# A two-layer graph attention kernel: superchunks of 26 chunks in place of 24, the carried row in row 0 of the node block, one scan penalty for all heads

## The chip, the core and the metric

The kernel runs on one core of one Trainium2 chip. The metric is the device time of one launch in microseconds (us); less is better. The engines are named as in the profile: PE (TensorE matmul; PEld is its weight load), DVE (VectorE), ACT (ScalarE), POOL (GpSimd) and SP (SyncE, which here issues nearly all plain DMAs). Ln is line n of the kernel before, unless the text says otherwise.

## What is computed

A graph with N = 6250 nodes of 256 features and E = 200000 edges, sorted by destination, each with 32 edge attributes. Two graph attention layers, with 4 heads of 64 and 1 head of 256, follow a layer norm with ReLU. The reference, cut:

```python
def _gat(x, src, dst, ea, Wg, a_s, a_d, Wge, a_e, b, n, h, f):
    hx = (x @ Wg).reshape(n, h, f)
    he = (ea @ Wge).reshape(-1, h, f)
    al = leaky_relu(einsum('nhf,hf->nh', hx, a_s)[src] + einsum('nhf,hf->nh', hx, a_d)[dst]
                    + einsum('ehf,hf->eh', he, a_e), 0.2)
    m = segment_max(al, dst, num_segments=n)
    al = exp(al - m[dst])
    al = al / segment_sum(al, dst, num_segments=n)[dst]
    out = segment_sum(hx[src] * al[:, :, None], dst, num_segments=n)
    return out.reshape(n, h * f) + b

# h = relu(layernorm(x)); each layer l, with self loops added to the edges (their edge term is
# the mean of te over the node's edges):
te = relu(edge_attr @ We_l + be_l) * exp(x @ Wo_l + bo_l)[src][:, None]
x0 = relu(_gat(h, ..., HEADS=4) + h);  x1 = _gat(x0, ..., 1) + x0;  result = x + x1 + h
```

## The kernel before, in words

**Tiles and steps.** The sorted edges are cut into 1563 chunks of 128 edges, and these into superchunks of C = 24 chunks (`cuts`, L46): 64 of 24, one of 14 and one of 13. One superchunk is one step of a layer, so there are 66 steps in layer 0 and 66 in layer 1. The nodes that a superchunk's edges lead to lie side by side and are fewer than 128, so a step owns a block of up to 128 node rows that begins at its first destination, `base`.

**The prologue** norms x, multiplies it by the layer's weights and writes the table T0: 268 numbers for each node, the row that an edge gathers. It works on groups of GT = 7 node tiles (after a first group of 2): DVE takes statistics, ACT norms (`h`, L303), PE turns and multiplies, DVE adds the bias into one of three `trow` buffers (L428), SP stores the group to T0 (L328). Step 0's 24 chunks are gathered from x itself, before T0 is there (`NX` = 24, L243). Between these lines a generator of index work is woven in; SP loads `drow` (L441), the destinations with one row per superchunk, and `r` (L443, tile `r4`), and DVE makes `lrow` from drow (L468), which goes to `locrow` in DRAM, and from r4 the link flags (L481 to L489).

**A step** (`edges`, L611 on) is an order written out by hand, and each engine runs its instructions in that order:

- POOL gathers the next step's G rows, one indirect DMA per chunk (`gather`, L928), with a memset of a tile `gap` after each (L932). G has three buffers, so gather(k+3) waits for the sums of step k.
- PE multiplies the edge attributes (y, L1014; ACT's ReLU R, L1019) and adds the destination term by a one-hot product (zad, L1028, L1073, L1087). DVE turns the result round (rt, L1101; ade, L1104), adds the gathered term (al, L1115 to L1121) and runs the maximum along each destination's edges: two scans along the chunk (L1128, L1130), whose penalties `pen` restart the scan where the destination changes, links over the partitions (L1148, L1150) and the maxima (L1165 to L1192).
- DVE scales G (L1223, 6.5 us) and builds the one-hot S from `loc`, the edge's destination less `base` (L1058, 3.3 us). PE then adds up S x G over the chunks, two matmuls each, into u (L1234), and ACT copies u to U (`evict`, L1239).
- A destination whose edges go on in the next superchunk must hand its partial sums over. `carry` (L1241) picks the last node's row of U with a matmul by the column `lsel` (PE fin, L1245) and copies it to row 0 of a tile (ACT, L1247); `carried` (L1197) adds it, rescaled, to the first edge of the next step before that step's sums.
- `finish` merges the self loop and normalizes. In layer 0, `rows1` to `rows3` multiply the block by the next layer's weights and store the 128 rows of table T1 (`t1row`, L1370). In layer 1 the block goes to the output (L1375), for the last two steps by an indirect DMA from POOL (L1379).
- `nodes` (L989) loads the block's own rows two steps ahead: `tw` from the table (L995), and in layer 0 also the x rows (L997). Edge attributes `ea` and the bytes `lb` come for two steps at once (L955), link flags `fl` for four (L980), indices `gi` for four (L554).

Neighbouring blocks overlap by the rows that do not belong to them; later stores overwrite these in order. Layer 1's first gather waits for the last T1 store. The last four steps of a layer run in two other orders (`tight`, `last`), in which no further gather of the same layer is left to wait for.

**Scan penalties.** `pen` holds 4 numbers for each chunk, one per head, all the same: DVE computes the first head's, and ACT copies it for the three others, once per group of four steps (L598).

Of the kernel before, what the change touches and what calls it, by code (L numbers as in the profile page):

```python
# [31 lines left out]
P = 128  # L32
C = 24
SE = P * C
NX = 24
D = 256
# [9 lines left out]
def cuts(E):  # L46

    n = -(-E // P)
    k = -(-n // C)
    if k == 1:  # L50
        return [n]
    rest = n - C * (k - 2)
    return [C] * (k - 2) + [rest - rest // 2, rest // 2]

# [24 lines left out]
class Kernel:  # L79
# [31 lines left out]
    def consts(self, wp):  # L111
# [35 lines left out]
        self.kps = k = self.ps_k.tile([P, 512], F32, name="kps")  # L147
        V.tensor_copy(k[:, 0:P], self.iota_f)
        m32 = wp.tile([P, 1], F32, name="m32", bufs=1)
# [6 lines left out]
        V.tensor_add(k[:, P:P + 1], self.iota_p, m32)  # L156
        self.k_iota, self.k_part, self.k_w = k[:, 0:P], k[:, P:P + 1], k[:, 2 * P:2 * P + 4 * C + 4]
        self.wea = []
# [38 lines left out]
    def prologue(self):  # L197
# [3 lines left out]
        NT = -(-N // P)  # L201
        GT = 7
        CX = self.CX = min(self.cs[0], NX)
# [226 lines left out]
    def indices(self, wp):  # L430
# [28 lines left out]
        self.qsel = cp.tile([P, NS, 4], F32, name="qsel")  # L459
        V.tensor_scalar(self.qsel.rearrange("p s k -> p k s"), qd, self.iota_p, None, op0=OP.add)  # L460
        yield
# [35 lines left out]
        yield  # L497
        ll = wp.tile([P, NS], F32, name="ll", bufs=1)
        V.tensor_sub(ll, last, base)
        self.lsel = cp.tile([P, NS], F32, name="lsel")  # L500
        V.tensor_scalar(self.lsel, ll, self.iota_p, None, op0=OP.is_equal)
        yield
# [6 lines left out]
        V.memset(chk, 0.0)  # L509
        V.tensor_scalar(chk[:, 0, :NS], ll[0:1, :], float(P - 1), None, op0=OP.is_gt)  # L510
        V.tensor_sub(qd[0:1], qlast[0:1], qbase[0:1])
# [5 lines left out]
        V.tensor_sub(nb[:, :NS], nb[:, 1:], nb[:, :NS])  # L517
        V.tensor_scalar(chk[:, 1, :NS], nb[:, :NS], float(P), None, op0=OP.is_gt)
        V.tensor_scalar(chk[:, 2, :NS], nb[:, :NS], 0.0, None, op0=OP.is_lt)
# [11 lines left out]
    def index_tiles(self):  # L531
        cp, cs, NS, NCH = self.cp, self.cs, self.NS, self.NCH

        self.groups = []
        for s in range(NS):
            g = self.groups[-1] if self.groups else None
            if g and cs[g[0]] == cs[s] and len(g) < 4:
                g.append(s)
            else:
                self.groups.append([s])  # L540
        self.src = cp.tile([P, NCH], I32, name="src")
        self.loc, self.fpen, self.lpen, self.isl = (cp.tile([P, NCH], BF, name=n)
                                                    for n in ("loc", "fpen", "lpen", "isl"))
        self.pen = cp.tile([P, 4 * NCH + 1], BF, name="pen")
        self.bad = cp.tile([P, 1 + len(self.groups)], F32, name="bad")
# [11 lines left out]
    def index_group(self, g, pool, di):  # L557
# [23 lines left out]
        for pen, e in zip((self.fpen, self.lpen), ends):  # L581
# [5 lines left out]
            yield  # L587
        pv = self.pen[:, 4 * o:4 * (o + w)].rearrange("p (s h c) -> p s h c", h=4, c=c)
        t = pool.tile([P, 4 * C], F32, name="gt", bufs=2)
# [3 lines left out]
        yield  # L593
        V.tensor_scalar(pv[:, :, 0, :], t3, 1.0, -BIG, op0=OP.min, op1=OP.mult)
        V.memset(self.pen[:, 4 * (o + w):4 * (o + w) + 1], -BIG)
        yield
        for h in range(1, 4):
            nc.scalar.activation(pv[:, :, h, :], pv[:, :, 0, :], AF.Copy)  # L598
            yield
        t = pool.tile([P, 4 * C], F32, name="gt", bufs=2)  # L600
# [10 lines left out]
    def edges(self, ctx):  # L611
# [12 lines left out]
        self.state = {0: None, 1: None}  # L624
        self.early = 0
        self.nodes(steps[0])
        self.gather(steps[0], self.CX)
# [16 lines left out]
        for k, st in enumerate(steps):  # L644
# [51 lines left out]
            if enter:  # L696
                pr = pv
            else:
                self.evict(st)
                self.carry(st)  # L700
                if pv:
                    self.rows1(pv)
                    late = pv
# [23 lines left out]
    def tight(self, st, pv, pr, nx):  # L727
# [38 lines left out]
        if final:  # L766
            self.carry(pv)
            drain(y)
            self.load_ea(st["k"] + 2)
        else:  # L770
            self.evict(pv)
        self.rphase2(nx)
        self.adst(nx)
        if not final:
            self.carry(pv)
            if pr:
                self.rows1(pr)
                self.rows2(pr)
# [10 lines left out]
    def last(self, st, pv, nx):  # L789
# [21 lines left out]
        if pv:  # L811
            self.evict(pv)
            self.carry(pv)
        drain(self.scale(st, 3))
# [174 lines left out]
    def nodes(self, st):  # L989
        nc, L, s = self.nc, st["L"], st["s"]  # L990
        r = self.row(0, s)
        tw = self.np_.tile([P, self.L[0].TW + D], F32, name="tw", bufs=5)
        st["tw"], st["xw"] = tw[:, :L.TW], tw[:, L.TW:L.TW + D]
        w = L.TW + L.l * D
        nc.sync.dma_start(tw[:, :w], self.T[L.l][ds(r, P), 0:w])  # L995
        if L.l == 0:
            nc.sync.dma_start(st["xw"], self.a["x"][ds(r, P), :])  # L997

# [6 lines left out]
    def rphase1(self, st):  # L1005
        nc, L = self.nc, st["L"]
        l, ea = L.l, st["ea"]
        st["R"] = R = self.wp.tile([P, 2, 32 * C], F32, name="R", bufs=1)
        c = st["C"]
        for i in range(2):  # L1010
            r = slice(i * PH, (i + 1) * PH)
            y = self.ps_y.tile([P, 1024], F32, name="y")
            for w, o in self.halves(st):
                nc.tensor.matmul(y[:, o], self.webd[l][r, :], ea[r, w], start=True, stop=True)  # L1014
            if c % 2:
                for w, o in self.halves(st):
                    nc.scalar.activation(R[:, i, w], y[:, o], AF.Relu, bias=self.be[l])
            else:
                nc.scalar.activation(R[:, i, :32 * c].rearrange("p (b n) -> p b n", b=2),  # L1019
                                     y.rearrange("p (b n) -> p b n", b=2)[:, :, :16 * c], AF.Relu, bias=self.be[l])  # L1020
            yield
# [9 lines left out]
    def spread(self, st):  # L1031
# [6 lines left out]
        if len(q) < 2 or q[0]["C"] != q[1]["C"]:  # L1038
# [5 lines left out]
        V.tensor_tensor(Q[:, :i].rearrange("p i (k j) -> p (i k) j", j=32),  # L1044
                        self.k_iota[:, 0:32].unsqueeze(1).to_broadcast([P, 4 * i, 32]),
                        self.qsel[:, s:s + i, :].rearrange("p i k -> p (i k)").unsqueeze(2)
# [4 lines left out]
    def onehots(self, st, c0=0, c1=C):  # L1051
        nc, o = self.nc, st["o"]
        c1 = min(c1, st["C"])
        if "S" not in st:
            st["S"] = self.sp.tile([P, C, P], F32, name="S")
        if c0 < c1:
            w = [P, c1 - c0, P]
# [3 lines left out]
    def parts(self, st):  # L1061
# [10 lines left out]
        st["zad"] = z = self.ps_1.tile([P, 1024], F32, name="zad")  # L1072
        self.nc.tensor.matmul(z[:, 400:400 + 3 * H], st["Q"], a3[:, :H, :].rearrange("p h t -> p (h t)"),  # L1073
                              start=True, stop=True)

    def blocks(self, st):
# [3 lines left out]
        self.nc.vector.tensor_tensor(aq[:, :, 4:4 + 3 * H],  # L1080
                                     st["zad"][:, 400:400 + 3 * H].unsqueeze(1).to_broadcast([P, 4, 3 * H]),
                                     self.quad.unsqueeze(2).to_broadcast([P, 4, 3 * H]), op=OP.mult)
# [24 lines left out]
    def logits(self, st):  # L1107
# [14 lines left out]
        yield  # L1122
        n, p0 = H * c, 4 * o
        fb, w = self.fb[st["k"] % 2], c if H > 1 else 1
        x = c - 1 + 32 * w
        st["f"], st["b"] = f, b = fb[:, :n], fb[:, x:x + n]
        st["ends"] = fb[:, c - 1:c + (31 + H) * w:w]
        V.tensor_tensor_scan(f, self.pen[:, p0:p0 + n], al[:, :n], -BIG, op0=OP.add, op1=OP.max)  # L1128
        yield
        V.tensor_tensor_scan(b[:, ::-1], self.pen[:, p0 + 1:p0 + n + 1][:, ::-1], al[:, :n][:, ::-1], -BIG,  # L1130
                             op0=OP.add, op1=OP.max)
# [65 lines left out]
    def carried(self, st):  # L1197


        if st["prev"] is not None:  # L1200
            L, V = st["L"], self.nc.vector
            H, pr = L.H, st["pr"]
            g, cv = st["G"][0:1, 0, :], st["prev"]["carry"]
            if H == 1:
# [31 lines left out]
    def evict(self, st):  # L1236
        L = st["L"]
        st["U"] = U = self.np_.tile([P, 272], F32, name="U", bufs=3)
        self.nc.scalar.activation(U[:, :L.W], st["u"][:, :L.W], AF.Copy)  # L1239

    def carry(self, st):  # L1241
        nc, L, s, U = self.nc, st["L"], st["s"], st["U"]
        if s + 1 < self.NS:
            pr = self.ps_f.tile([P, 512], F32, name="fin")
            nc.tensor.matmul(pr[0:1, :L.W], self.lsel[:, s:s + 1], U[:, :L.W], start=True, stop=True)  # L1245
            st["carry"] = cv = self.wp.tile([1, 272], F32, name="carry")
            nc.scalar.activation(cv[:, :L.W], pr[0:1, :L.W], AF.Copy)  # L1247

# [116 lines left out]
    def rows3(self, st):  # L1365
        nc, L, s = self.nc, st["L"], st["s"]
        if L.l == 0:
            self.table_row(st)
            r = self.row(0, s)
            nc.sync.dma_start(self.T[1][ds(r, P), :], st["trow"])  # L1370
            return
        o, out = st["o"], self.a["out"]
        if s < self.direct:
            r = self.row(1, s)
            nc.sync.dma_start(out[ds(r, P), :], o)  # L1375
        else:
            idx = self.np_.tile([P, 1], I32, name="oidx")
            nc.vector.tensor_add(idx, self.base_f[:, s:s + 1], self.iota_p)
            nc.gpsimd.indirect_dma_start(  # L1379
# [217 lines left out]
```

## Time and profile before

| | before |
|---|---|
| time, median of 3 runs (lowest to highest) | 4717.75 us (4715.25 to 4721.8) |
| profiled execution: its own time / its span | 4718.23 / 4716.0 us |
| granted TensorE clock, mean of the span | 0.732 |
| busy: PE / DVE / POOL / ACT | 3214.2 / 2878.5 / 3701.8 / 574.2 us |
| DMA, software queue (gathers) / hardware queue (SP) | 422.75 / 158.16 MB, 33.8% / 10.1% of 16 engines' span |
| first gather from T0 / first U / first gather of layer 1 / last U | 95.31 / 184.88 / 2419.91 / 4701.13 us |

Times of single instructions count from the start of the span. A group's line in the profile gives count, busy us and mean ns of one, then how long the engine was idle before these instructions and what ended most of that. "remote" is a releaser that the profile can't name, "issue" is time in which the engine waited for nothing that the profile shows. SPq rows are SP's DMA issues: start, how long the issue took, and what is moved.

### The profile page before, as it was taken

To read this page: it belongs to the slowest core of one execution; us is meant where nothing else is said; L and a number is where in the kernel's file an instruction comes from. 1 tells how busy PE (TensorE), PEld (TensorE's weight loads), DVE (VectorE), ACT (ScalarE), POOL (GpSimd) and SP (SyncE) were. 2 spreads that over 40 slices of the span, in tenths; PEclk is the share of its full clock that TensorE was granted. 3 is DMA by queue.
4 is the path that set the end of the run, shared out by engine and by line. 5 is a ranking of instruction groups with operands and counts; after the bars stand their busy time and mean duration, and the time that the engine had idled before them with its cause. 6 is when DMAs were issued, how large, how long until landed. Compare 5 with 4: busy or idle time off the path is not lost.

```text
span 4716.0 us, 38255 instructions
## 1 busy us (share of the span) xinstructions
PE 3214.2 (68%) x10176; PEld 1915.8 (41%) x10176; DVE 2878.5 (61%) x6552; ACT 574.2 (12%) x1282; POOL 3701.8 (78%) x6350
## 2 busy tenths in 40 slices
PE   7777767777677776777655666666666666656666
PEld 6444444444444443444422333434333343433334
DVE  7566767667676676766743555546455555645555
ACT  5111111111111111111100001000000100000010
POOL 5688888888888888888648888888888888888884
PEclk9677777767777777777866677777767776777778
DMA  6344444444444444444323444444444444444442
GB/s 216 111 129 126 136 122 129 134 122 135 127 134 127 124 136 123 132 131 124 107 84 104 128 118 126 125 112 127 120 127 118 126 126 111 127 118 128 118 124 63
DMA packets 236364, 584.09 MB, mean 124 GB/s; under 512 B 63097, under 2 KB 91007, under 8 KB 236073
## 3 DMA queue, kind: packets, MB, share of 16 engines
q0 software_dynamic: 150144, 422.75, 33.8%
q1 hardware_dynamic: 85579, 158.16, 10.1%
q8 instruction: 82, 1.34, 0.1%
q14 instruction: 143, 1.17, 0.1%
q10 hardware_dynamic: 416, 0.67, 0.1%
HBM read 547.11 MB, written 34.33 MB: 123 GB/s over the span
## 4 chain that ended last, share of the span: by engine, by line
DVE 40%; another core or an unknown queue 33%; PE 16%; issue 6%; ACT 4%; POOL 0%; DMA 0%; SPq 0%; DVEq 0%; ACTq 0%; POOLq 0%
DVE G L1223 16%; DVE S L1058 8%; PE y L1014 8%; PE fin L1245 3%; DVE rt L1101 2%; ACT R L1019 1%; ACT U L1239 1%; DVE ade L1104 1%; PE fin L1329 1%; PE u L1234 1%; PE lf L1138 1%; PE zad L1028 1%; DVE mt L1172 1%; DVE m L1175 1%
## 5 line engine op out<-in xcount | busy, mean ns | idle before, releaser
L928 POOL DMA_INDIRECT G<-T,src x3102 | 2974.0, 959 | 938.3 <-issue 498.2
L1234 PE MATMUL u<-G,S 128*128 128x270 f32 (+1 forms) x6252 | 1469.7, 393 | 110.3 <-issue 58.0
L1234 PEld LDWEIGHTS u<-G,S 128*128 128x128 f32 x6252 | 1186.9, 192 | 394.5 <-issue 87.1
L1245 PE MATMUL fin<-U,lsel 128*1 128x270 f32 (+1 forms) x260 | 132.8, 613 | 1143.3 <-ACT U L1239 1136.6
L1223 DVE TENSOR_TENSOR G<-G,kps 128x6144 f32<-128x6144 f32 (+2 forms) x140 | 853.3, 6100 | 0.0
L1014 PE MATMUL y<-ea,webd 64*128 64x384 f32 (+1 forms) x1056 | 754.6, 866 | 89.2 <-issue 65.5
L932 POOL MEMSET gap<- 128x128 f32 x3102 | 684.6, 221 | 4.3 <-remote 1.3
L1148 DVE TENSOR_TENSOR_SCAN cl<-fl,cl,lf 4x129 f32<-4x129 f32 (+1 forms) x130 | 61.2, 471 | 1016.6 <-PE zad L1073 994.3
L1245 PEld LDWEIGHTS fin<-U,lsel 128*1 128x1 f32 x260 | 11.1, 81 | 1202.6 <-ACT U L1239 1201.5
L1028 PE MATMUL zad<-R,wea 128*64 128x384 f32 (+1 forms) x1056 | 474.0, 816 | 0.3 <-DVE aq L1080 0.3
L1014 PEld LDWEIGHTS y<-ea,webd 64*128 64x128 f32 x1056 | 303.3, 317 | 360.3 <-issue 330.0
L1058 DVE TENSOR_TENSOR S<-kps,loc 128x3072 f32<-128x3072 f32 x132 | 436.2, 3305 | 0.0
L1019 ACT ACTIVATE R<-y,webd 128x768 f32<-128x768 f32 x260 | 232.9, 896 | 794.6 <-PE y L1014 348.3
L1028 PEld LDWEIGHTS zad<-R,wea 128*64 128x64 f32 x1056 | 160.4, 207 | 314.9 <-issue 248.5
L1239 ACT ACTIVATE U<-u 128x270 f32<-128x270 f32 (+1 forms) x132 | 51.8, 393 | 1627.1 <-remote 1585.4
L1101 DVE STREAM_TRANSPOSE rt<-zad 128x768 f32<-128x768 f32 (+1 forms) x130 | 125.0, 961 | 27.8 <-remote 15.7
L424 PE MATMUL fin<-wg,h1T 128*128 128x260 f32 x264 | 135.7, 669 | 3.2 <-ACT h1T L1331 3.2
L1043 DVE TENSOR_TENSOR lb<-lb,kps 128x1536 bf16<-128x1536 bf16 (+1 forms) x68 | 113.0, 1662 | 0.0
L424 PE MATMUL ps<-wg,hT 128*128 128x266 f32 x292 | 89.8, 435 | 25.4 <-ACT hT L311 13.9
L424 PEld LDWEIGHTS fin<-wg,h1T 128*128 128x128 f32 x264 | 76.0, 317 | 53.7 <-issue 36.3
L1272 ACT ACTIVATE mw<-mw,mg 128x2 f32<-128x2 f32 x66 | 19.7, 298 | 557.3 <-DVE mw L1264 249.1
L1138 PE MATMUL lf<-ident,fb 128*36 128x128 f32 (+1 forms) x132 | 54.9, 416 | 42.8 <-DVE al L1119 28.2
(193 smaller groups left out, 2269.0 us busy)
## 6 DMA issues: line engine op xcount, KB each, us to landing
G<-T,src POOLq DMA_INDIRECT x3102
ea<-in_ea_dram SPq DMA_DIRECT2D x64, 768.0 KB
lb<-locrow SPq DMA_DIRECT2D x64, 384.0 KB
T<-t1row SPq DMA_DIRECT2D x66, 260.0 KB
tw<-T SPq DMA_DIRECT2D x66, 258.0 KB
tw<-T SPq DMA_DIRECT2D x66, 134.0 KB
tw<-in_x_dram SPq DMA_DIRECT2D x66, 128.0 KB
out_dram<-fb SPq DMA_DIRECT2D x64, 128.0 KB
```

What stands on the lines that cost most here:

```text
L424: self.nc.tensor.matmul(ps[:, :L.MW], hT[:, k, :], self.wg[L.l][:, k, :], start=(k == 0), stop=(k == 1))
L928: nc.gpsimd.indirect_dma_start(out=G[:, c, 0:L.TW], out_offset=None, in_=self.rows[L.l][0:n * (1 + L.l), :], in_offset=bass.IndirectOffset ...
L932: nc.gpsimd.memset(self.gap, 0.0)
L1014: nc.tensor.matmul(y[:, o], self.webd[l][r, :], ea[r, w], start=True, stop=True)
L1019: nc.scalar.activation(R[:, i, :32 * c].rearrange("p (b n) -> p b n", b=2), y.rearrange("p (b n) -> p b n", b=2)[:, :, :16 * c], AF.Relu, ...
L1028: nc.tensor.matmul(st["zad"][i * PH:(i + 1) * PH, o], self.wea[l][0], R[:, i, w], start=True, stop=False)
L1043: V.tensor_tensor(lb[:, :, :n], lb[:, :, :n], self.k_part.unsqueeze(2).to_broadcast([P, i, n]), op=OP.is_equal)
L1058: nc.vector.tensor_tensor(st["S"][:, c0:c1, :], self.k_iota.unsqueeze(1).to_broadcast(w), self.loc[:, o + c0:o + c1].unsqueeze(2).to_broad ...
L1101: V.transpose(rv[:, :32 * c].rearrange("p (b n) -> p b n", b=2), z.rearrange("p (b n) -> p b n", b=2)[:, :, :16 * c])
L1223: nc.vector.tensor_tensor(v, v, pw[:, c0:c1, :].unsqueeze(3) .to_broadcast([P, c1 - c0, H, L.F]), op=OP.mult)
L1234: nc.tensor.matmul(st["u"][:, :L.W], S[:, i, :], G[:, i, 0:L.W], start=(j == 0), stop=(j == c - 1))
L1245: nc.tensor.matmul(pr[0:1, :L.W], self.lsel[:, s:s + 1], U[:, :L.W], start=True, stop=True)
```

## The change

- `C` is 26. `cuts` fills superchunks of 26 and splits what is left: 59 of 26, one of 15, one of 14; 61 steps per layer.
- Column 0 of the one-hot S now stands for the superchunk's last node: a 128x1 copy writes `lastloc` of the step into column 0 of the comparison row, and columns 1 to 127 compare with j - 1. So row 0 of U is the carried row, `carried` reads it there, and `carry` and `lsel` are gone. A block's nodes are rows 1 to 127, and its DMAs (`tw`, x, T1 store, output) move 127 rows. Row 0 of the four `tw` buffers (there were five) is set to zero once.
- `pen` holds one number per chunk. In each step of layer 0 an ACT copy spreads it over the four heads into `pen4`; the three copies per group (L598) are gone.
- With it go `GT` = 6 in the prologue, a column offset in `zad` (480 for 400), and row 0's index out of bounds in the last two outputs. `NX` stays 24, so two of step 0's 26 chunks are gathered from T0. The loads and tiles with one row per superchunk have 61 rows for 66.

```diff
-C = 24
+C = 26
@@ cuts
-    k = -(-n // C)
-    if k == 1:
-        return [n]
-    rest = n - C * (k - 2)
-    return [C] * (k - 2) + [rest - rest // 2, rest // 2]
+    k = n // C
+    rest = n - C * k
+    if rest < 8:
+        k, rest = k - 1, rest + C
+    return [C] * k + [rest - rest // 2, rest // 2]
@@ prologue
-        GT = 7
+        GT = 6
@@ index_tiles
-        self.pen = cp.tile([P, 4 * NCH + 1], BF, name="pen")
+        self.pen = cp.tile([P, NCH + 1], BF, name="pen")
...
+        self.pen4 = [cp.tile([P, 4 * C + 1], BF, name=f"pen4{i}") for i in range(2)]
@@ index_group
-        for h in range(1, 4):
-            nc.scalar.activation(pv[:, :, h, :], pv[:, :, 0, :], AF.Copy)
-            yield
@@ edges, tight, last
-                self.carry(st)
...
+        self.tws = [self.np_.tile([P, self.L[0].TW + D], F32, name=f"tw{i}", bufs=1) for i in range(4)]
+        for t in self.tws:
+            nc.vector.memset(t[0:1, :], 0.0)
@@ nodes
-        tw = self.np_.tile([P, self.L[0].TW + D], F32, name="tw", bufs=5)
+        tw = self.tws[st["k"] % 4]
...
-        nc.sync.dma_start(tw[:, :w], self.T[L.l][ds(r, P), 0:w])
+        nc.sync.dma_start(tw[1:P, :w], self.T[L.l][ds(r, P - 1), 0:w])
...
-            nc.sync.dma_start(st["xw"], self.a["x"][ds(r, P), :])
+            nc.sync.dma_start(st["xw"][1:P, :], self.a["x"][ds(r, P - 1), :])
@@ rphase1
+        if H > 1:
+            st["pen"] = pen = self.pen4[st["k"] % 2]
+            nc.scalar.activation(pen[:, :H * c].rearrange("p (h c) -> p h c", c=c),
+                                 self.pen[:, o:o + c].unsqueeze(1).to_broadcast([P, H, c]), AF.Copy)
+            if c < C:
+                nc.vector.memset(pen[:, H * c:H * c + 1], -BIG)
@@ onehots
             st["S"] = self.sp.tile([P, C, P], F32, name="S")
+            nc.vector.tensor_copy(self.k_iota[:, 0:1], self.lastloc[:, st["s"]:st["s"] + 1])
@@ carried
-            g, cv = st["G"][0:1, 0, :], st["prev"]["carry"]
+            g, cv = st["G"][0:1, 0, :], st["prev"]["U"]
@@ carry (removed)
-            nc.tensor.matmul(pr[0:1, :L.W], self.lsel[:, s:s + 1], U[:, :L.W], start=True, stop=True)
-            st["carry"] = cv = self.wp.tile([1, 272], F32, name="carry")
-            nc.scalar.activation(cv[:, :L.W], pr[0:1, :L.W], AF.Copy)
@@ rows3
-            nc.sync.dma_start(self.T[1][ds(r, P), :], st["trow"])
+            nc.sync.dma_start(self.T[1][ds(r, P - 1), :], st["trow"][1:P, :])
...
-            nc.sync.dma_start(out[ds(r, P), :], o)
+            nc.sync.dma_start(out[ds(r, P - 1), :], o[1:P, :])
```

More of the change, by code (lines that the diff above doesn't have):

```diff
@@ L147, in consts @@
         self.kps = k = self.ps_k.tile([P, 512], F32, name="kps")
-        V.tensor_copy(k[:, 0:P], self.iota_f)
+        V.tensor_scalar(k[:, 0:P], self.iota_f, -1.0, None, op0=OP.add)
+        V.tensor_copy(k[:, P + 2:P + 34], self.iota_f[:, 0:32])
+        self.iota_m = cp.tile([P, 1], F32, name="iota_m")
+        nc.gpsimd.iota(self.iota_m, pattern=[[0, 1]], base=-1, channel_multiplier=1,
+                       allow_small_or_imprecise_dtypes=True)
         m32 = wp.tile([P, 1], F32, name="m32", bufs=1)
@@ L156, in consts @@
         V.tensor_add(k[:, P:P + 1], self.iota_p, m32)
-        self.k_iota, self.k_part, self.k_w = k[:, 0:P], k[:, P:P + 1], k[:, 2 * P:2 * P + 4 * C + 4]
+        self.k_iota, self.k_part, self.k_32 = k[:, 0:P], k[:, P:P + 1], k[:, P + 2:P + 34]
+        self.k_w = k[:, 2 * P:2 * P + 4 * C + 4]
         self.wea = []
@@ L459, in indices @@
         self.qsel = cp.tile([P, NS, 4], F32, name="qsel")
-        V.tensor_scalar(self.qsel.rearrange("p s k -> p k s"), qd, self.iota_p, None, op0=OP.add)
+        V.tensor_scalar(self.qsel.rearrange("p s k -> p k s"), qd, self.iota_m, None, op0=OP.add)
         yield
@@ L497, in indices @@
         yield
-        ll = wp.tile([P, NS], F32, name="ll", bufs=1)
+        self.lastloc = ll = cp.tile([P, NS], F32, name="lastloc")
         V.tensor_sub(ll, last, base)
-        self.lsel = cp.tile([P, NS], F32, name="lsel")
-        V.tensor_scalar(self.lsel, ll, self.iota_p, None, op0=OP.is_equal)
         yield
@@ L509, in indices @@
         V.memset(chk, 0.0)
-        V.tensor_scalar(chk[:, 0, :NS], ll[0:1, :], float(P - 1), None, op0=OP.is_gt)
+        V.tensor_scalar(chk[:, 0, :NS], ll[0:1, :], float(P - 2), None, op0=OP.is_gt)
         V.tensor_sub(qd[0:1], qlast[0:1], qbase[0:1])
@@ L517, in indices @@
         V.tensor_sub(nb[:, :NS], nb[:, 1:], nb[:, :NS])
-        V.tensor_scalar(chk[:, 1, :NS], nb[:, :NS], float(P), None, op0=OP.is_gt)
+        V.tensor_scalar(chk[:, 1, :NS], nb[:, :NS], float(P - 1), None, op0=OP.is_gt)
         V.tensor_scalar(chk[:, 2, :NS], nb[:, :NS], 0.0, None, op0=OP.is_lt)
@@ L543, in index_tiles @@
                                                     for n in ("loc", "fpen", "lpen", "isl"))
-        self.pen = cp.tile([P, 4 * NCH + 1], BF, name="pen")
+        self.pen = cp.tile([P, NCH + 1], BF, name="pen")
+        self.nc.gpsimd.memset(self.pen[:, NCH:], -BIG)
+        self.pen4 = [cp.tile([P, 4 * C + 1], BF, name=f"pen4{i}") for i in range(2)]
+        for t in self.pen4:
+            self.nc.gpsimd.memset(t[:, 4 * C:], -BIG)
         self.bad = cp.tile([P, 1 + len(self.groups)], F32, name="bad")
@@ L587, in index_group @@
             yield
-        pv = self.pen[:, 4 * o:4 * (o + w)].rearrange("p (s h c) -> p s h c", h=4, c=c)
         t = pool.tile([P, 4 * C], F32, name="gt", bufs=2)
@@ L593, in index_group @@
         yield
-        V.tensor_scalar(pv[:, :, 0, :], t3, 1.0, -BIG, op0=OP.min, op1=OP.mult)
-        V.memset(self.pen[:, 4 * (o + w):4 * (o + w) + 1], -BIG)
+        V.tensor_scalar(self.pen[:, o:o + w], t[:, :w], 1.0, -BIG, op0=OP.min, op1=OP.mult)
         yield
-        for h in range(1, 4):
-            nc.scalar.activation(pv[:, :, h, :], pv[:, :, 0, :], AF.Copy)
-            yield
         t = pool.tile([P, 4 * C], F32, name="gt", bufs=2)
@@ L766, in tight @@
         if final:
-            self.carry(pv)
             drain(y)
@@ L774, in tight @@
         if not final:
-            self.carry(pv)
             if pr:
@@ L812, in last @@
             self.evict(pv)
-            self.carry(pv)
         drain(self.scale(st, 3))
@@ L1008, in rphase1 @@
         st["R"] = R = self.wp.tile([P, 2, 32 * C], F32, name="R", bufs=1)
-        c = st["C"]
+        c, o, H = st["C"], st["o"], L.H
+        st["pen"] = self.pen[:, o:o + c + 1]
+        if H > 1:
[4 more added lines that the diff above has]
+                nc.vector.memset(pen[:, H * c:H * c + 1], -BIG)
         for i in range(2):
@@ L1044, in spread @@
         V.tensor_tensor(Q[:, :i].rearrange("p i (k j) -> p (i k) j", j=32),
-                        self.k_iota[:, 0:32].unsqueeze(1).to_broadcast([P, 4 * i, 32]),
+                        self.k_32.unsqueeze(1).to_broadcast([P, 4 * i, 32]),
                         self.qsel[:, s:s + i, :].rearrange("p i k -> p (i k)").unsqueeze(2)
@@ L1072, in parts @@
         st["zad"] = z = self.ps_1.tile([P, 1024], F32, name="zad")
-        self.nc.tensor.matmul(z[:, 400:400 + 3 * H], st["Q"], a3[:, :H, :].rearrange("p h t -> p (h t)"),
+        self.nc.tensor.matmul(z[:, 480:480 + 3 * H], st["Q"], a3[:, :H, :].rearrange("p h t -> p (h t)"),
                               start=True, stop=True)
@@ L1080, in blocks @@
         self.nc.vector.tensor_tensor(aq[:, :, 4:4 + 3 * H],
-                                     st["zad"][:, 400:400 + 3 * H].unsqueeze(1).to_broadcast([P, 4, 3 * H]),
+                                     st["zad"][:, 480:480 + 3 * H].unsqueeze(1).to_broadcast([P, 4, 3 * H]),
                                      self.quad.unsqueeze(2).to_broadcast([P, 4, 3 * H]), op=OP.mult)
@@ L1122, in logits @@
         yield
-        n, p0 = H * c, 4 * o
+        n = H * c
+        pen = st["pen"]
         fb, w = self.fb[st["k"] % 2], c if H > 1 else 1
@@ L1127, in logits @@
         st["ends"] = fb[:, c - 1:c + (31 + H) * w:w]
-        V.tensor_tensor_scan(f, self.pen[:, p0:p0 + n], al[:, :n], -BIG, op0=OP.add, op1=OP.max)
+        V.tensor_tensor_scan(f, pen[:, :n], al[:, :n], -BIG, op0=OP.add, op1=OP.max)
         yield
-        V.tensor_tensor_scan(b[:, ::-1], self.pen[:, p0 + 1:p0 + n + 1][:, ::-1], al[:, :n][:, ::-1], -BIG,
+        V.tensor_tensor_scan(b[:, ::-1], pen[:, 1:n + 1][:, ::-1], al[:, :n][:, ::-1], -BIG,
                              op0=OP.add, op1=OP.max)
@@ L1239, in evict @@
         self.nc.scalar.activation(U[:, :L.W], st["u"][:, :L.W], AF.Copy)
[L1241 to L1245, printed above, removed]
-            st["carry"] = cv = self.wp.tile([1, 272], F32, name="carry")
-            nc.scalar.activation(cv[:, :L.W], pr[0:1, :L.W], AF.Copy)
     def merge(self, st, wp, w):
@@ L1374, in rows3 @@
             r = self.row(1, s)
-            nc.sync.dma_start(out[ds(r, P), :], o)
+            nc.sync.dma_start(out[ds(r, P - 1), :], o[1:P, :])
         else:
             idx = self.np_.tile([P, 1], I32, name="oidx")
-            nc.vector.tensor_add(idx, self.base_f[:, s:s + 1], self.iota_p)
+            nc.vector.tensor_add(idx, self.base_f[:, s:s + 1], self.iota_m)
+            nc.vector.memset(idx[0:1, :], 1 << 20)
             nc.gpsimd.indirect_dma_start(
```

## The prediction

> **What bounds the kernel now.** I read the busy times first, then the waits, then one step of the timeline, then the order of SP's transfers. The page's first section and three of its groups (columns: count, busy us and mean ns, idle us before them with its releaser):
>
> ```profile
> PE 3214.2 (68%) x10176; PEld 1915.8 (41%) x10176; DVE 2878.5 (61%) x6552; ACT 574.2 (12%) x1282; POOL 3701.8 (78%) x6350
> ...
> L928 POOL DMA_INDIRECT G<-T,src x3102 | 2974.0, 959 | 938.3 <-issue 498.2
> ...
> L1245 PE MATMUL fin<-U,lsel 128*1 128x270 f32 (+1 forms) x260 | 132.8, 613 | 1143.3 <-ACT U L1239 1136.6
> ...
> L932 POOL MEMSET gap<- 128x128 f32 x3102 | 684.6, 221 | 4.3 <-remote 1.3
> ```
>
> POOL is the busiest. Its gathers cost 0.95 us, the gap memset 0.22 and the issue 0.17, 1.34 us a chunk. The waits of POOL and ACT (us in total, times, longest):
>
> ```profile
> POOL G L928 <- remote: 285.9, 120, 3.0
> POOL G L928 <- DMA T<-t1row: 69.1, 1, 69.1
> ...
> ACT U L1239 <- remote: 1585.4, 123, 58.5
> ```
>
> The 120 "remote" waits are one pause of about 2.4 us at each step's turn. The timeline shows that turn, on POOL, PE and ACT:
>
> ```profile
> 823.12 11.37 PE L1234 MATMUL u<-G,S 128*128 128x270 f32 x48 [0.49 <-issue]
> 842.61 0.61 PE L1245 MATMUL fin<-U,lsel 128*1 128x270 f32 x1 [8.12 <-ACT U L1239]
> ...
> 839.64 0.23 POOL L932 MEMSET gap<- 128x128 f32 x1
> 842.40 0.95 POOL L928 DMA_INDIRECT G<-T,src  x1 [2.54 <-remote]
> ...
> 842.16 0.40 ACT L1239 ACTIVATE U<-u 128x270 f32<-128x270 f32 x1 [9.65 <-remote]
> ```
>
> The one-hot sums are done at 834.5, yet U is copied at 842.16, 2.3 us after POOL's last memset; then POOL starts again. U follows POOL's running group and not PE's sums: a full step takes 34.60 us in layer 0 and 34.40 in layer 1, although layer 1 has 4 us less PE work and 2.4 less DVE work. So gathers pace the steps, and PE's chain has some 7.7 us (layer 0) and 10.3 us (layer 1) to spare.
>
> **Part 1: longer steps, fewer of them.** A layer had 64 steps of 24 chunks and then 14 and 13; it now has 59 of 26 and then 15 and 14. The gathers stay 3126 chunks at 1.34 us; only the pause can shrink. U comes 34.36 us after the group's first gather with 24 chunks, 18.70 with the 13 of the last step: 1.424 us a chunk and 0.19 fixed, and 0.24 more to the next first gather. So 26 chunks give 37.45 us: 59 x 37.45 against 64 x 34.60 is -4.8, and the tail's two extra chunks cost +2.8, so -2.0. Layer 1 (34.16 and 18.58) gives -2.2. Together **-4**. If instead the pause is a constant 2.4, a step is 34.60 + 2 x 1.336 = 37.27, and the two layers win 12.8 + 11.8 = 25. I take -4, which rests on two group sizes, and keep -25 for the range.
>
> **Part 2: the carried row.** PE's fin (two matmuls, 1.07 us) and ACT's copy (0.39) go. In a full step they lie inside the spare 7.7 us and are worth nothing. In the last four steps of a layer POOL runs dry and the chain sets the pace: 8 steps, of whose 1.46 us between a sixth and a half lies on it, **-4** (-2 to -6).
>
> **Part 3: small operations.** Added per step: one 128x1 DVE copy, about 0.14 us by L1258's row; per layer-0 step one ACT copy of the penalties, 0.27 by L598's. ACT is 12% busy and DVE's step has 12 us idle. One-hots and scale grow by 26/24 (3.3 to 3.6 and 6.5 to 7.1). All lie under the spare 7.7; without that cover they would cost about 1.3 us a step. Zero. Step 0 gathers two chunks more from T (2.7 us), inside POOL's 9.8 us wait for U at 185.62.
>
> **Part 4: 127 and 61 rows.** The node transfers (tw, x, the T1 store, the output) now have 127 rows, and the loads with one row per superchunk (`drow`, `r4`, `bcol`) 61 instead of 66. The trace's transfer records show how rows spread. 128 rows of 1072 B ran in 0.8 us, 16 or more at once; `r4`'s 66 rows ran at most 11 at once; but the 106-row zero store (L235) began with a row every 45 ns, one after another, and took 3.84 us. Row counts with small divisors get few engines: 128 has 16, 66 has 11, 106 has 2; 127 and 61 are prime. I take one engine for both. The Trainium skill, "DMA: Bandwidth & Descriptors", section "Why a DMA increments its semaphore by 16 and not by 1", says just this: the largest number up to 16 that divides the dimension, with 127 rows on 1 as an example, always the lowest-numbered engine. By it every one of these transfers shares one engine; the 106 rows agree.
>
> On one engine, by rows of this trace (46 ns for 1024 B, 48 for 1072, 85 for 2080): tw 6.1 us, x 5.8, T1 store 10.8 in layer 0; tw 10.8 and out 5.8 in layer 1. Four costs follow.
>
> *Prologue.* SP's order there:
>
> ```profile
> 30.05 0.35 SPq L441 DMA_DIRECT2D drow<-in_drow_dram  x1
> 30.44 0.34 SPq L443 DMA_DIRECT2D r<-in_prow_dram  x1
> ...
> 35.14 0.34 SPq L328 DMA_DIRECT2D T<-trow  x1
> 35.58 0.38 SPq L218 DMA_DIRECT2D x<-in_x_dram  x1
> ```
>
> A `drow` row of 12288 B took 460 ns at best, 775 in the mean. 61 rows of 13312 B one behind another are 30 to 51 us; `r4` adds 61 x 0.155 to 0.19, 10 to 12 us. What SP queues behind them (a T0 store, x tiles) has a share on that engine, and lands only at 76 to 100. DVE, which computes lrow from drow at 46.89 (L468), stops there; then the trow buffer of the store issued at 35 is wanted again for tile 18, which DVE wrote at about 51.6. That is 24 to 48 us late; some 5 us of ACT's waits for POOL's ln values vanish in the stall: 19 to 48. The other engines' transfers end early, so rows should run near their best: **+28**. The gathers of T wait for this chain (ACT h, at 95.31), so nothing hides it.
>
> *Start.* tw and x for steps 0 to 2 leave at 143.7 to 147.3. The first lands 6.1 instead of 0.8 us after its start, and DVE's parts(0) reads it at 145.87: +5 to +9, **+6**.
>
> *Layer boundary.* POOL waits 69.1 us for the last T1 store, issued at 2417.05 and 12 us after the one before it; the gather starts at 2419.91. 10.8 instead of 1.0 us: **+10**.
>
> *Full steps.* In a layer-0 step this engine has 22.7 us of node rows, 1.6 of other loads, and its share of 26 gathers, two packets each: 8.6 us at 166 ns, the fastest, 13 at the mean 250, 21 at 410, the slowest tenth. That is 33 to 46 us in a step of 37.45: from nothing to 8.6 us a step, 0 to 470 for 55 steps. The transfers themselves are wanted 33 us (fl) to 47 (tw) after their issue, and POOL may run 8 gathers ahead, so lateness is hidden until the engine is full. At the mean packet it is just full: 0.3 us a step, **+16**. Layer 1 (16.6 us of rows) has room.
>
> **The sum.** Own time 4718.23 us (span 4716.0 and 2.2 around it), 0.5 above the median of the runs. -4 - 4 + 28 + 6 + 10 + 16 = +52: **4770**.
>
> **The rivals.** *Faster: the rows are spread all the same.* If 127 rows get 16 engines in shares of 8 and 7, as 128 do, part 4 falls away and 4689 (constant pause) to 4710 is left. For it: SP's queue never shows an engine number. Against: the 106 rows. It decides as soon as tw lands within 2 us.
>
> *The one engine overflows.* If gather packets on it take the loaded 410 ns, gathers of layer 0 wait for its share and a step takes 46 us: 4754 + 55 x 8.6, about 5230; at 300 ns (15.6 us of gathers, 39.9 in all) 2.5 us a step, 4890. Against: the mean of 250, and a slowed engine leaves fewer packets in flight elsewhere.
>
> *The pause is constant.* 4749 with the other terms, 4721 if these are at their low ends (19, 5, 10, 0, and -6 for the tails). For it: the pause is 2.45 and 2.36 us in both layers.
>
> *PE or DVE becomes the bound.* It would need 7.7 us of growth in a layer-0 step; the sums' two chunks add 0.95, y and zad about 0.4, DVE 0.9. Against.
>
> **How the numbers follow.** Forecast 0.48 (4735 to 4800); overflow 0.18 (4800 to 5230); constant pause with low costs 0.16 (4715 to 4735); rows spread 0.14 (4689 to 4710); PE or DVE 0.04. About 0.2% (9.4 us) is what a measurement of this kernel can tell from no change. Faster: the 0.14 and a little of the constant pause, 0.17. Same: most of the rest of that case, 0.10. Slower 0.73. The range leaves out the lower half of the spread case and the overflow beyond 4880: 4700 to 4880, about 0.8.
>
> **What would show it.** Right: a tw transfer that takes 6 us with its rows one after another; DVE waiting at lrow or trow near 50 to 80 us for a DMA, and POOL's first gather from T near 123; the boundary's wait 10 us longer than the stores explain before; full steps near 37.5 us, with U still 0.2 us before POOL's restart; no fin at L1245. Wrong: layer-0 steps beyond 38 us or clearly longer than layer 1's (the engine overflows); steps at 37.27 or below (constant pause); a first gather still near 95 us (rows spread, or the stall hidden).

## The result: 4800 us for 4717, slower by 1.8%

The changed kernel takes 4800.13 us (median of 4 runs, 4796.63 to 4809.32), the kernel before 4717.47 (4 runs): ratio 1.0179, 95% interval 1.0164 to 1.0194, or +82.7 us. The forecast was 4770, the range 4700 to 4880. The profiled execution is the slowest of the four, 4809.32 us; its span of 4807.3 is 91.3 longer than that of before. In the lines of a run, Ln is a line of that run's own kernel (L1244 here is L1234 before).

The page after, the same groups as before; `fin` at the carry is gone, and POOL's work is what it was:

```profile
PE 3025.5 (63%) x9676; PEld 1849.1 (38%) x9676; DVE 2812.9 (59%) x6213; ACT 490.0 (10%) x1093; POOL 3703.0 (77%) x6382
...
L929 POOL DMA_INDIRECT G<-T,src x3102 | 2967.4, 957 | 981.9 <-issue 512.1
...
L933 POOL MEMSET gap<- 128x128 f32 x3100 | 685.5, 221 | 9.4 <-remote 6.2
```

The waits after, of POOL, ACT and DVE:

```profile
POOL G L929 <- remote: 226.2, 91, 3.7
POOL G L929 <- DMA T<-t1row: 91.4, 1, 91.4
...
POOL G L929 <- ACT G L327: 25.3, 1, 25.3
...
ACT U L1249 <- remote: 1718.8, 93, 58.6
...
DVE a L1077 <- DMA tw<-T: 32.9, 2, 28.6
...
DVE lrow L473 <- DMA drow<-in_drow_dram: 21.4, 1, 21.4
...
DVE trow L433 <- DMA T<-trow: 10.4, 1, 10.4
...
DVE cl L1158 <- DMA fl<-flags: 9.5, 1, 9.5
```

The pause at a step's turn is still there, but rarer. POOL's wait for the last T1 store has grown from 69.1 to 91.4 us. New among the longer waits are DVE's for `drow`, for a T0 store and for the flags `fl`, and POOL's, 25.3 us, for an exp of ACT at the prologue's end. DVE's longest wait for a `tw` load, at the layer boundary, has grown from 3.1 to 28.6 us, but the first U of layer 1 does not come later for it: it follows the layer's first gather by 109.9 us, and by 110.8 in the split version below, where that wait is 4.8.

The timeline of one full step of layer 0, on PE, POOL and ACT:

```profile
922.54 12.12 PE L1244 MATMUL u<-G,S 128*128 128x270 f32 x52 [0.75 <-DVE G L1223]
...
945.49 0.22 POOL L933 MEMSET gap<- 128x128 f32 x1
948.46 0.95 POOL L929 DMA_INDIRECT G<-T,src  x1 [2.75 <-remote]
...
948.22 0.40 ACT L1249 ACTIVATE U<-u 128x270 f32<-128x270 f32 x1 [15.74 <-remote]
```

The sums end at 934.7, U comes at 948.22: 13.5 us now lie between them (7.7 before), so in a full step neither the larger operations nor the missing carry are on the path. SP's issues in the prologue (start, how long the issue took):

```profile
31.57 0.60 SPq L446 DMA_DIRECT2D drow<-in_drow_dram  x1
32.21 1.34 SPq L448 DMA_DIRECT2D r<-in_prow_dram  x1
33.60 33.55 SPq L449 DMA_DIRECT2D src<-in_src_dram  x1
...
71.67 1.16 SPq L333 DMA_DIRECT2D T<-trow  x1
72.88 0.75 SPq L223 DMA_DIRECT2D x<-in_x_dram  x1
```

The issue behind the two 61-row loads took 33.55 us, and the T0 store that left at 35.14 before leaves at 71.67. In the transfer records drow's 61 rows run from 35.25 to 72.78, 553 ns each, never more than two at once; the 127 rows of a tw load of layer 0 take 8.3 us in the median (5.8 to 8.7), those of a T1 store 14.4.

By stages, from the copies of U (us; the last three columns are from one other chip, on which the kernel before takes 4768; the split version is experiment 1's):

| stage | before | after | before | after | split |
|---|---|---|---|---|---|
| first gather from T0 | 95.3 | 135.2 | 94.8 | 132.3 | 103.8 |
| to the first U | 184.9 | 238.0 | 184.6 | 236.2 | 205.8 |
| first to last U of layer 0 | 2217.6 | 2212.6 | 2239.6 | 2236.9 | 2231.2 |
| to the first U of layer 1 | 119.5 | 140.1 | 120.0 | 141.1 | 130.3 |
| first to last U of layer 1 | 2179.2 | 2201.4 | 2201.7 | 2196.4 | 2193.6 |
| rest | 14.9 | 15.2 | 15.1 | 15.0 | 15.2 |

So +53.1 at the start, -4.9 in layer 0, +20.6 at the boundary and +22.2 in layer 1. In layer 0 the fewer, longer steps have paid 5 us; the losses lie at the start, at the boundary and in layer 1. On the other chip layer 1 has no such loss (-5.3).

### The profile page after: what moved, and what is told of

Its sections match the earlier page's. It is cut to its first block, busy times and chain, and to the rows that moved or that the text cites. A ratio compares the mean times of both kernels' runs of the same rounds, so it can differ in the third digit from the quotient of the medians.

```text
span 4807.3 us, 36571 instructions
## 1 busy us (share of the span) xinstructions
PE 3025.5 (63%) x9676; PEld 1849.1 (38%) x9676; DVE 2812.9 (59%) x6213; ACT 490.0 (10%) x1093; POOL 3703.0 (77%) x6382
## 4 chain that ended last, share of the span: by engine, by line
DVE 32%; POOL 24%; another core or an unknown queue 20%; issue 11%; PE 8%; DMA 2%; SPq 1%; ACT 1%; DVEq 0%; POOLq 0%; ACTq 0%
POOL G L929 20%; DVE G L1233 10%; DVE S L1067 5%; POOL gap L933 5%; PE u L1244 4%; PE y L1022 2%; DVE rt L1110 1%; DVE lb L1051 1%; DMA G<-T,src 1%; SPq L449 1%; DVE G L1124 1%; PE zad L1036 1%; DVE cl L1158 1%; DVE al L1128 1%
## 5 line engine op out<-in xcount | busy, mean ns | idle before, releaser
L1244 PE MATMUL u<-G,S 128*128 128x270 f32 (+1 forms) x6252 | 1533.0, 403 | 253.4 <-issue 124.4
L1244 PEld LDWEIGHTS u<-G,S 128*128 128x128 f32 x6252 | 1222.8, 198 | 568.3 <-DVE G L1223 169.4
L1233 DVE TENSOR_TENSOR G<-G,kps 128x6656 f32<-128x6656 f32 (+2 forms) x130 | 851.6, 6556 | 0.0
L1022 PE MATMUL y<-ea,webd 64*128 64x416 f32 (+2 forms) x976 | 659.7, 811 | 102.9 <-issue 58.9
L1165 PE MATMUL lf<-ident,cl 36*128 36x36 f32 (+1 forms) x122 | 37.2, 305 | 902.4 <-DVE cl L1160 848.4
L1036 PE MATMUL zad<-R,wea 128*64 128x416 f32 (+2 forms) x976 | 465.7, 857 | 19.4 <-issue 17.4
L1067 DVE TENSOR_TENSOR S<-kps,loc 128x3328 f32<-128x3328 f32 (+2 forms) x122 | 436.0, 3574 | 4.2
L1022 PEld LDWEIGHTS y<-ea,webd 64*128 64x128 f32 x976 | 246.9, 279 | 313.7 <-issue 251.5
L1027 ACT ACTIVATE R<-y,webd 128x832 f32<-128x832 f32 x240 | 227.5, 948 | 497.9 <-PE y L1022 282.8
L1110 DVE STREAM_TRANSPOSE rt<-zad 128x832 f32<-128x832 f32 x120 | 122.9, 1024 | 106.8 <-remote 92.5
L1082 PE MATMUL zad<-a,Q 128*128 128x12 bf16 (+1 forms) x122 | 22.2, 182 | 234.6 <-DVE a L1080 200.9
L1051 DVE TENSOR_TENSOR lb<-lb,kps 128x1664 bf16<-128x1664 bf16 (+1 forms) x64 | 112.4, 1756 | 2.2 <-issue 2.2
```

The costliest lines, as they stand in the source:

```text
L1036: nc.tensor.matmul(st["zad"][i * PH:(i + 1) * PH, o], self.wea[l][0], R[:, i, w], start=True, stop=False)
L1051: V.tensor_tensor(lb[:, :, :n], lb[:, :, :n], self.k_part.unsqueeze(2).to_broadcast([P, i, n]), op=OP.is_equal)
L1067: nc.vector.tensor_tensor(st["S"][:, c0:c1, :], self.k_iota.unsqueeze(1).to_broadcast(w), self.loc[:, o + c0:o + c1].unsqueeze(2).to_broad ...
L1110: V.transpose(rv[:, :32 * c].rearrange("p (b n) -> p b n", b=2), z.rearrange("p (b n) -> p b n", b=2)[:, :, :16 * c])
L1233: nc.vector.tensor_tensor(v, v, pw[:, c0:c1, :].unsqueeze(3) .to_broadcast([P, c1 - c0, H, L.F]), op=OP.mult)
L1244: nc.tensor.matmul(st["u"][:, :L.W], S[:, i, :], G[:, i, 0:L.W], start=(j == 0), stop=(j == c - 1))
```

## The experiments

Each kernel ran beside the kernel before on the same chip, and each set on another: 4378.4 us for the kernel before in the first set (1 to 4), 4767.6 in the second (5 to 8), 4379.9 in the third (9 to 12). So ratios are what is compared between sets, and of the expectations in us, which were made with the times of the pair's chip, the differences.

**1 to 4: which rows, which place.** In the split version each 127-row DMA goes as 112 + 15 rows and each 61-row one as 60 + 1:

```diff
-        nc.sync.dma_start(tw[1:P, :w], self.T[L.l][ds(r, P - 1), 0:w])
+        for i, j in ((1, 113), (113, P)):
+            nc.sync.dma_start(tw[i:j, :w], self.T[L.l][ds(r, P - 1), 0:w][i - 1:j - 1, :])
...
-        nc.sync.dma_start(drow, a["drow"])
+        for i, j in ((0, NS - 1), (NS - 1, NS)):
+            nc.sync.dma_start(drow[i:j], a["drow"][i:j])
```

> The changed kernel, but each DMA of 127 rows goes as two of 112 and 15, each of 61 rows as 60 and 1. If one engine for 127 and 61 rows is the cause (theory A): first gather from T0 near 97 us (135 in the changed kernel), U(0) near 200, layer boundary 122 for 140, no long steps in layer 1, 4700 to 4710 us in all, a little faster than the kernel before. If the longer steps or the new order at the start are the cause (theory B): above 4770.

Measured 4399.9 us, 1.0048 (1.0031 to 1.0064) of the kernel before. drow's rows now ran from 26.3 to 31.3, up to 17 at once, and the first gather came at 97.1, as theory A says. That it is still slower than the kernel before was not expected.

> Only the 61-row DMAs of the prologue are split into 60 and 1; the node DMAs keep 127 rows. Theory A: the first gather comes back to about 97 us, U(0) to about 205, the rest stays as in the changed kernel: 4800 - 35 to 40 = 4760 to 4765. Theory B: unchanged, 4800.

Measured 4481.6, 1.0234 (1.0217 to 1.0251): with the prologue mended and the node rows on one engine it is 81.7 us slower than the split version. First gather at 98.0, as expected; the price of the node rows is far above the 16 + 10 + 6 that the prediction had: 62.8 us more in layer 0, 15.4 at the boundary and 5.1 by the first U.

> Only the node DMAs are split into 112 and 15 rows; the 61-row DMAs stay. Theory A: the first gather stays at 135, U(0) some 8 us earlier than 238, boundary 122, layer 1 without long steps: 4735 to 4750. Theory B: unchanged, 4800.

Measured 4427.3, 1.0115 (1.0098 to 1.0132): 27.4 us slower than the split version, all of it by the first gather (126.8 for 97.1). So on this chip the one engine costs 27 with the prologue's loads and 82 with the node rows.

The fourth is the changed kernel with 24 chunks:

```diff
-C = 26
+C = 24
```

> The changed kernel with C = 24: 66 superchunks per layer again (66-row loads in the prologue), the node DMAs with 127 rows, no carry matmul. Theory A: first gather near 97, boundary longer than before's 119.5 by 15 to 20, some long steps in layer 1: 4745 to 4765. If the carry's removal is worth something in full steps, layer-0 steps fall below 34.6; I expect 34.6. Theory B (longer steps are what costs): back to 4718.

Measured 4568.7, 1.0435 (1.0417 to 1.0452), the slowest of all: a miss. With 24 chunks and no pause a step has 24 x 1.34 = 32.2 us. By the prediction's rates the one engine has 32 to 36 us of rows and gather packets in it, and the node rows did take 22.8 us a step in this trace (22.7 in the prediction); so here the engine overflows. From this kernel's waits of DVE:

```profile
DVE G L1124 <- DMA G<-T,src: 664.3, 78, 15.3
DVE gf L578 <- DMA gi<-in_dnx_dram: 269.8, 17, 18.4
DVE lb L1051 <- DMA lb<-locrow: 138.2, 15, 12.1
```

and from SP's timeline in one of its steps:

```profile
574.44 16.13 SPq L996 DMA_DIRECT2D tw<-T  x1
590.81 11.21 SPq L998 DMA_DIRECT2D tw<-in_x_dram  x1
604.66 4.71 SPq L1372 DMA_DIRECT2D T<-t1row  x1
```

SP sits 16 and 11 us in issues that take 0.3 us when the engine is free, and the small loads behind them (`gi` every four steps, `lb` every two) come late. The wait for G is no loss by itself: in the split version it is 1063 us, since the gathers set the pace. Layer 0's full steps average 34.4 us; with 126 rows (experiment 12) they average 31.8.

**5 to 8: the same chip for all, and the steps by themselves.**

> The kernel before, unchanged, for a trace from the same chip as the three runs beside it: as the chip goes, 4378 or 4717 us. If its full steps are 24 x 1.34 = 32.2 us long with no pause of 2.4 us, then longer steps have nothing to win there; if they are 34.6 they have 0.27 x 24 / 26 of a us per chunk pair at most, some 25 us in all.

Measured 4763.2. Its full steps are 34.94 and 34.73 us.

> The changed kernel, unchanged, beside the runs of its parts. Theory A (one engine): the two losses found by parts add up, 38 for the prologue's loads and 60 to 80 for the node rows, on top of what the split version has: ratio 1.018 to 1.030. First gather 25 to 40 us later than in the kernel before.

Measured 4826.2, 1.0118 (1.0101 to 1.0135), less than expected: the parts did not cost here what they cost in the first set, and layer 1 has one step that is 1.4 us longer, where on the chip of the pair six pairs of steps were longer, by 31.6 us together.

> The version with 112 + 15 and 60 + 1 rows, beside the changed kernel. Theory A: 80 to 110 us faster than the changed kernel; against the kernel before 0.995 to 1.005.

Measured 4783.4, 1.0033 (1.0022 to 1.0044): 42.8 us faster than the changed kernel, half of the 80 to 110 expected, and 15.8 slower than the kernel before. Its full steps are 37.81 and 37.55 us: two more chunks cost 2.87 and 2.82, 1.43 and 1.41 a chunk, near the forecast's 1.424 and above the 1.34 of a constant pause.

Experiment 8 is the split version with C = 24.

> C = 24 with the same 112 + 15 rows (and 65 + 1 in the prologue): the carried row and the penalties alone, without longer steps and without the one engine. If longer steps help, this is 4 to 25 us slower than the split version with C = 26; if POOL is busy throughout, the two are within 5 us. The carried row itself: within 5 us of the kernel before.

Measured 4790.4, 1.0042 (1.0025 to 1.0059). Layer 0's 60 full steps take 2100.0 us, 2097.6 in the kernel before on this chip: the carry was worth nothing there. Beside the split version with C = 26 it is 7.0 us slower, within the 4 to 25 for longer steps that help, though the two intervals overlap. It was to be within 5 us of the kernel before and is 22.8 slower. In the profiled runs layer 1 takes 10.4 us more, which is not explained, and the first U is 15.4 us late, with neither longer steps nor one engine in the kernel. POOL's timeline, first in the kernel before (experiment 5):

```profile
94.77 1.29 POOL L928 DMA_INDIRECT G<-T,src  x1 [18.01 <-ACT h L303]
```

and then here:

```profile
131.11 1.06 POOL L933 DMA_INDIRECT G<-T,src  x1 [42.76 <-ACT G L327]
```

Step 1's gathers wait for the last exp of the prologue; in the kernel before they wait for `h`, which reads the x tiles. They fill the second G buffer. By the order in which the kernel opens its pools this buffer takes the place of the prologue's x tiles, and of the work tiles behind them if it is larger. 24 chunks are 24 x 270 x 4 = 25920 B a partition, 26 are 28080. With GT = 7 the four x tiles are 28672 B, and both sizes fit; with GT = 6 they are 24576, and both reach into the work tiles. That is theory L, the third.

**9 to 12: the layout, and the best of the parts.** In 9 and 10:

```diff
-        GT = 6
+        GT = 7
```

> The changed kernel with GT = 7 in place of 6, nothing else. If step 1's gathers start late because their buffer (28080 B a partition) no longer fits over the x tiles of the prologue (4 x 6 KB, before 4 x 7 KB) and so waits for the tiles behind them (theory L, layout), POOL's 25 us wait for ACT's last exp goes, and U(0) comes 12 to 25 us earlier: ratio to the kernel before 1.008 to 1.014. If the late start only follows from the late T0, nothing changes: 1.012 to 1.018.

Measured 4496.5, 1.0263 (1.0249 to 1.0277), outside what was expected: this chip has no pause, as in the first set, and the changed kernel itself was not run on such a one. POOL's wait for the exp is gone (step 1's gathers follow the first one, at 119.5, without it), as theory L says, but with the one engine left, DVE waits 247.1 us for `gi` as in experiment 4.

> The split version (112 + 15 and 60 + 1 rows) with GT = 7. Theory L: 12 to 25 us faster than the split version, ratio to the kernel before 0.998 to 1.001, U(0) near 187. Otherwise 1.003 to 1.005, U(0) near 205.

Measured 4368.0, 0.9972 (0.9961 to 0.9984): faster than the kernel before. From 1.0048 to 0.9972 is 33 us for GT, more than expected. It fits a POOL that never pauses: step 1's gathers begin 35.0 us earlier, and nearly all of that comes through to the end. They begin in experiment 1, and then here, at:

```profile
124.93 0.94 POOL L933 DMA_INDIRECT G<-T,src  x1 [25.29 <-ACT G L327]
```

```profile
89.92 0.95 POOL L933 DMA_INDIRECT G<-T,src  x1 [0.30 <-ACT hT L316]
```


Experiment 11 moves 126 rows in one DMA each:

```diff
-        nc.sync.dma_start(tw[1:P, :w], self.T[L.l][ds(r, P - 1), 0:w])
+        nc.sync.dma_start(tw[1:P - 1, :w], self.T[L.l][ds(r, P - 2), 0:w])
```

> C = 26, GT = 7, the node DMAs with 126 rows in one DMA each (14 x 9; blocks are limited to 126 nodes), 61-row loads as 60 + 1. If only the number of engines matters (theory A), as fast as the split version with GT = 7 or 2 to 5 us faster, since SP issues half as many node DMAs: ratio 0.996 to 1.000.

Measured 4363.9, 0.9962 (0.9949 to 0.9976), the lowest ratio of all, within the interval of experiment 10. 126 rows of 2080 B landed in 1.1 us. The Trainium skill, "DMA: Bandwidth & Descriptors", section "Why a DMA increments its semaphore by 16 and not by 1", gives 14 engines to 126 rows and 1 to 127 by its divisor rule; the 1.1 us here and the 61 and 127 rows one after another above agree. POOL's waits in this kernel:

```profile
POOL G L933 <- DMA T<-t1row: 61.3, 1, 61.3
POOL out_dram L1386 <- DVE oidx L1385: 18.5, 1, 18.5
POOL G L933 <- DMA T<-trow: 17.9, 1, 17.9
```

> The same with C = 24: the carried row and the penalties without longer steps. If longer steps are worth 4 us, ratio 0.998 to 1.001; if 25, about 1.003 to 1.005 beside 0.996 to 1.000 of C = 26. Full steps of layer 0 as long as in the kernel before, since the carry was hidden there.

Measured 4366.2, 0.9966 (0.9954 to 0.9978): the same as with 26 chunks within the intervals. Where POOL does not pause, longer steps are worth nothing that this can tell (2.3 us).

## Why the prediction was right, and where it was not

**The mechanism was right, and it was not the only one.** One engine for 127 and 61 rows was the larger part of the loss: 42.8 of 58.6 us in the second set. In the profiled runs of that chip, changed less split is 30.4 us to the first U, 5.7 in layer 0, 10.8 at the boundary and 2.8 in layer 1. The other 15.8 stay in the split version. Most of its loss is the late start that `GT` = 6 brings (experiments 8 to 10), for which the prediction had no term; that GT = 7 takes it away where POOL pauses was not tried. On the pair's own chip no mended kernel was run, so how its 82.7 us divide is not measured.

**The number was partly luck.** +52 was forecast and +82.7 measured. A cost that did not come in the pair (+16 in full steps) stood in for part of two that nobody had forecast (`GT`, and layer 1's long steps).

**Steps, -4: small, as forecast.** With 26 chunks the split version is 7.0 us faster than with 24 (experiments 7 and 8), and 2.3 where POOL does not pause (11 and 12). The stage table cannot tell it better: the split version wins 8.4 and 8.1 us in the two layers, but three groups of two more chunks, 6 x 1.34 = 8.0 us, are gathered ahead of each layer's first U. At the boundary they are 8.3 of the +10.3; at the start they cannot be told from the late gathers.

**Carry, -4 in the tails: not confirmed.** With C = 24 split, layer 0's tail took 143.8 us for 142.0 and layer 1's 122.4 for 115.5.

**Prologue, +28: right.** DVE waited for drow until 73.4 and for the T0 store until 84.4; the forecast's 30 to 51 us of rows give 62 to 83 for the first, and 76 to 100 was its range for the second. With all else the same the one engine made the first gather 28.6 us later (second set) and 29.7 (first set). What the forecast did not have is that SP itself is held, 33.55 us. In the pair the gather is 39.9 us late; some 9 of that are in the split version too (second set), and GT = 7 took 10.0 away (experiment 10 against 1).

**Start, +6: somewhat less.** Changed less split is 28.6 at the first gather and 30.4 at the first U; in the first set the node rows cost 0.9 and 5.1 at the same places.

**GT = 6, put at nothing: the step that failed.** The first U is 53.1 us late, the forecast had 34. The missing 19 are in the split version as well (21.2 in the second set): its step 1's gathers begin 36.8 us later than before, after the wait for the exp. The prediction did not cost `GT` at all: a size in another stage decided what a buffer has to wait for.

**Boundary, +10: right.** From the last U of layer 0 to layer 1's first gather it is 17.5 us before and 30.3 after, and 19.5 in the split version: 10.8 by the one engine. In layer 0's tail the prediction missed +10: the step before the last took 46.5 us for 36.2, because SP's two T1 stores held up the `fl` load that DVE's links needed. In the split version it takes 36.5.

```profile
2404.50 13.81 SPq L1372 DMA_DIRECT2D T<-t1row  x2
2418.40 4.33 SPq L981 DMA_DIRECT2D fl<-flags  x2
```

**Full steps, +16: too much for the pair, too little for others.** Layer 0's step is 37.32 us, below the 37.45 without any contention. The node rows took 23.2 us of it (22.7 in the forecast), and between 300 and 2390 us DVE waited for no DMA longer than 3 us. The overflow rival was wrong here. It was right in experiments 2, 4 and 9, where POOL does not pause and a step is shorter: 26 x 1.34 = 34.8 us, or 32.2 with 24 chunks.

**The constant pause: not settled by the steps' length.** It gives 2.67 us more a step, the forecast 2.85. The pair's steps grew by 2.72 and 2.81, those of the split version by 2.87 and 2.82. But the 25 us that it promised did not come: longer steps were worth 7.0.

**Open: layer 1 of the pair.** Five pairs of steps there took 5.4 to 6.7 us more than two normal ones, a sixth 1.5, 31.6 in all: more than the layer's +22.2. The second set's run of the same kernel has one step that is 1.4 us longer. Why they come and go, and whether the one engine has a part in them, is not settled.

The other rivals fell: the rows were not spread, and PE's sums ended 13.5 us ahead of U in a full step.

## What to carry to other kernels

Look at the row count of every transfer that an edit touches, the rare ones too: 127 and 61 rows ran one after another, two at once at most, and 126 or 60 + 1 ran up to 17 at once. A slow transfer's price is in what the queue holds up behind it, so price the small loads that follow. When a tile in one stage changes size, check which tile of the next stage takes its place, and what that one now waits for.

## What was not expected of the hardware

**SP is held, not only the data.** The issue of `src` took 33.55 us (0.41 before) while the 61 rows of `drow`, issued ahead of it, ran one after another; the issues of unrelated transfers behind it waited in line.

**The pause goes with the chip.** Where the kernel before takes 4718 and 4768 us, ACT's copy of U waits for a "remote" signal at most steps and POOL pauses there. In the sets where it takes 4378 and 4380, the same wait is released by PE, and POOL has no such pause. (The kernel before itself has a trace only from the first two; the granted clock was 0.73 on these, 0.76 on the others.) ACT's waits in experiment 11:

```profile
ACT U L1253 <- PE u L1248: 525.5, 122, 21.1
```

Gathers cost 0.96 us on all of them. What the "remote" signal is, and why only the slower chips show it, no run here tells. How much the changes cost went with it: the one engine lost 43 us where POOL pauses, and where it does not 27 with the prologue's loads and 82 with the node rows.
